# Masked attention over a sparse adjacency on one core: ScalarE's passes over three adj tiles, one search, one list of keys and one score put at other places in the order

## The chip, the cores and the metric

The kernel runs on one core of one Trainium2 chip. The metric is the device time in microseconds; lower is better. The kernel before took 669.54 us (median of three runs, 668.49 to 670.58). The program writes the order of work of ScalarE and VectorE by hand, and that of GpSimd in the first part; the order of the other queues (PE, the DMA queue of SyncE, GpSimd later) is made by a scheduler from the program's order and from what is ready.

## The reference

```python
h = relu(layernorm(x))                    # x: 2708 x 1024
q = h @ W_q.T + b_q;  k = h @ W_k.T + b_k;  v = h @ W_v.T + b_v
z = (q @ k.T) / 32
z = where(z * adj == 0, -10000, z * adj)  # adj: 2708 x 2708, 0 or 1, one in 677 set
out = x + relu(softmax(z) @ v)
```

A row of adj has four ones on average, so nearly all of the score matrix is masked.

## The kernel before

**Tiles and units.** The 2708 rows are 22 tiles of 128 (tile 21 has 20). The kernel first forms M, the product of the two score weights, on PE (lines 388 to 536). Then come 20 units, n = 0 to 19, of two tiles each: units 0 to 9 form score rows q = h M, units 10 to 19 the outputs from the summed rows u. One unit is a 2 x 2 block product with seven block multiplications of 8 matmuls each (`multiply`, `add_block` L909), and takes PE some 25.8 us. Within a unit, `after(i)` for i = 0 to 6 runs between the blocks: there the program places all other work. The results leave PSUM through ScalarE copies (L922, L925, L955, L987, L998) and VectorE sums (L990, L993 for q; L1020, L1024 for the outputs); the next unit's rows are transposed on PE (L359), copied by ScalarE (L649) and combined by VectorE (L653).

**The adj tiles.** Each is loaded by SyncE (L317, 1354 KB) into one of three buffers, tile t into buffer t mod 3. Three things are then done to it:

- `counted(t)` (L320, the pass): ScalarE adds up |adj| over each row (L324), the number of ones that the keys are held against at the end;
- `found(t)` (L326, the search): VectorE finds the places of the ones, four FIND_INDEX8 of 685 columns (L334);
- `listed(t)` (L336, the keys): for the last tile of a batch ((8..11), (16..19), (20), (21) are batches), VectorE turns the places of the batch into keys (L346 to L352).

The buffer is free for tile t + 3 when both the pass and the search have ended.

**The steps.** `steps_at[n, i]` (L700) is a string of steps that `follow` (L272) carries out in that order at `after(i)` of unit n. "p16" is the pass over tile 16, "i19" the search alone, "j19" the keys alone, "f16" search and keys (the keys only at a batch's end), "e9" pass, search and keys; the first step that names a tile asks for its load. "s", "r", "a", "h", "k" and "+" are steps of the layer norm of x: statistics on VectorE, root on GpSimd, application on ScalarE (L250), storing of h and the column sum on GpSimd. "c" is `counts(0, 11)`, "o" is `sort(0, 11)`, "w" writes the first table with GpSimd and ends GpSimd's order by hand (L297).

**Counts and sort.** `counts(11, 22)` runs at (3, 2): VectorE forms `hot` (L604) from the keys. `sort(11, 22)` at (3, 3) begins with two products of `hot` on PE (`ps_in` L615, `ps_all` L617), which stand in PE's queue ahead of a block of unit 3, and brings the rows in order of their number of ones, so that tile t needs only K[t] slots.

**Attention.** From unit 5 on, a generator, `attention` (L855), gives VectorE's steps for the sorted tiles in the order 8, 7, 6, 5, 4, 3, 2, 0, 1, 9, 15, 14, 13, 12, 16, 17, 20, 10, 18, 19, 11, and `advance` (L898) takes some 20 us of them per unit, by the costs that the steps yield. For a tile: `scores` (L784) is K[t] instructions L790, each on one gathered row of h (gathers by GpSimd, L545) and the tile's q rows; behind the last one, the q rows of the following tile are fetched. `weights` (L809) makes the softmax weights in a few small VectorE instructions (L832 to L834; L819 to L828 for tiles 10 and 20, which can hold rows without ones) and ends in one ScalarE instruction, the first term (L835; L829 for tiles 10 and 20). `sums` (L839) adds the other terms on VectorE (L843), and its first one waits for ScalarE. Where two neighbouring tiles have at most 12 slots together, two scores of the next tile go ahead of the weights and the rest between weights and sums. K is 2 for tiles 9, 10 and 20.

Of the kernel before, what the change touches and what calls it, by code (L numbers as in the profile page):

```python
# [39 lines left out]
def slot_counts(n, count):  # L40


    nodes = 2708
    pmf = [math.comb(nodes, k) * RATE**k * (1 - RATE) ** (nodes - k) for k in range(SLOTS + 1)]
    counts = []
    for t in range(count):
        k = 1
        while k < SLOTS:
            above = max(0.0, 1.0 - sum(pmf[: k + 1]))
            if n * above < 0.01 if t == 0 else n * above + 4 * math.sqrt(n * above * (1 - above)) <= t * P:  # L50
                break
            k += 1
        counts.append(k)
    return counts
# [3 lines left out]
def tile_preln_masked_attention(  # L58
# [24 lines left out]
    K = slot_counts(EARLY * P, EARLY) + slot_counts(N - EARLY * P, FULL - EARLY) + [0]  # L83
# [597 lines left out]
    def natural_rows(n):  # L681
# [15 lines left out]
    nc.vector.tensor_scalar(large[:, 0:1], large[:, 0:1], 10000.0, None, op0=ALU.is_gt)  # L697
    nc.vector.tensor_scalar(large[:, 1:2], large[:, 1:2], 250000.0 / D, None, op0=ALU.is_gt)

    steps_at = {(0, 0): "s4-5 e9", (0, 1): "r4 +0 +1 +2 f10", (0, 3): "p10 i11", (0, 4): "j11 a4 p11", (0, 5): "h4 +3 s6-7 e12",  # L700
                (0, 6): "r6 f13", (1, 1): "f14", (1, 2): "p13 a6", (1, 3): "h6 s8-9 p14", (1, 4): "r8 p15 i15", (1, 5): "j15",
                (1, 6): "f16 c", (2, 1): "f17", (2, 2): "p16 a8", (2, 3): "r10 f18 p17 w h8",
                (2, 4): "a10 p18", (2, 5): "f19 k10", (2, 6): "f20 f21 p19", (3, 2): "p20", (3, 3): "p21"}
    steps_ahead = {(2, 2): "o s10"}

    slots, free = [], []
# [44 lines left out]
    def ask(t):  # L751

        g_of[t] = []
        wanted.extend((t, s) for s in range(K[t]))

    def fetch(t):

        assert t in formed
        if t not in g_of:
            ask(t)  # L760
        tq[t] = work.tile([P, D], FT, tag="hT", name=f"pq_{t}", bufs=2)
        if t < EARLY:
            got = gather(tq[t], q_dram[:, :], t, SLOTS, P)
            if t == order[0]:
                first_q.append(got)
        else:
            nc.gpsimd.dma_start(tq[t], q_late[(t - EARLY) * P:(t - EARLY + 1) * P, :])

    def fill():
        while wanted and free:  # L770
            t, s = wanted.pop(0)
            g = free.pop(0)
            with tc.issue_after(first_q[0].ins) if first_q else nullcontext():
                gather(g, h_dram[:, :], t, s, P, skip=True)
            g_of[t].append(g)
# [8 lines left out]
    def scores(t, then):  # L784
        k = K[t]
        at[t] = list(range(k))
        for s in range(k):
            fill()
            junk = work.tile([P, D], mybir.dt.uint8, tag="junk", name="junk2", bufs=1)
            chained(lambda: nc.vector.scalar_tensor_tensor(  # L790
                junk, g_of[t][s], 1.0, tq[t], op0=ALU.mult, op1=ALU.mult, accum_out=zall[:, t, s:s + 1]))
            if s < k - WIDE:
                free.append(g_of[t][s])
            yield 1.3
        tq.pop(t)
        if k > WIDE:

            g_of[t] = g_of[t][k - WIDE:]
            wanted.extend((t, s) for s in range(k - WIDE))
            at[t] = list(range(k - WIDE, k)) + list(range(k - WIDE))  # L800
        if then is not None:
            fetch(then)
        fill()
        w = stat.tile([P, SLOTS + 1], FT, tag="w", name=f"w_{t}")
        if t not in EMPTY:
            nc.scalar.activation(w[:, :k], zall[:, t, 0:k], AF.Exp)
        ws[t] = w

    def weights(t):  # L809

        k = K[t]
        z, ok = zall[:, t, 0:k], valid[:, t, 0:k]
        w = ws.pop(t)
        m = stat.tile([P, 4], FT, tag="m", name=f"m_{t}")
        coef = stat.tile([P, SLOTS], FT, tag="coef", name="coef")
        u = row_tile(f"u_{t}")
        if t in EMPTY:
            assert summed
            nc.vector.memset(w[:, 0:1], MASKED)  # L819
            nc.vector.tensor_scalar(coef[:, :k], ok, -1.0, -MASKED, op0=ALU.add, op1=ALU.mult)  # L820
            nc.vector.tensor_mul(w[:, 1:1 + k], z, ok)
            nc.vector.tensor_add(w[:, 1:1 + k], w[:, 1:1 + k], coef[:, :k])
            nc.vector.tensor_reduce(m[:, 0:1], w[:, 0:1 + k], AX.X, ALU.max, negate=True)
            nc.scalar.activation(w[:, 0:1 + k], w[:, 0:1 + k], AF.Exp, bias=m[:, 0:1], accum_out=m[:, 1:2])
            nc.vector.scalar_tensor_tensor(m[:, 2:3], w[:, 0:1], float(N - 1 - k), m[:, 1:2], op0=ALU.mult, op1=ALU.add)
            nc.vector.reciprocal(m[:, 3:4], m[:, 2:3])
            nc.vector.tensor_scalar(coef[:, :k], w[:, 1:1 + k], w[:, 0:1], m[:, 3:4], op0=ALU.subtract, op1=ALU.mult)
            nc.vector.tensor_mul(m[:, 2:3], w[:, 0:1], m[:, 3:4])  # L828
            nc.scalar.activation(u, hsum, AF.Copy, scale=m[:, 2:3])  # L829
        else:  # L830
            with tc.issue_after(chain[-1].ins):
                nc.vector.scalar_tensor_tensor(w[:, :k], w[:, :k], 1.0, ok, op0=ALU.mult, op1=ALU.mult, accum_out=m[:, 1:2])  # L832
                nc.vector.reciprocal(m[:, 3:4], m[:, 1:2])
                chain.append(nc.vector.tensor_scalar(coef[:, :k], w[:, :k], m[:, 3:4], None, op0=ALU.mult))  # L834
            nc.scalar.activation(u, g_of[t][0], AF.Copy, scale=coef[:, at[t][0]:at[t][0] + 1])  # L835
            free.append(g_of[t][0])
        us[t] = u, coef

    def sums(t):  # L839
        u, coef = us.pop(t)  # L840
        for s in range(0 if t in EMPTY else 1, K[t]):
            fill()
            chained(lambda: nc.vector.scalar_tensor_tensor(  # L843
                u, g_of[t][s], coef[:, at[t][s]:at[t][s] + 1], u, op0=ALU.mult, op1=ALU.add))
            free.append(g_of[t][s])
            yield 1.3
        fill()
        g_of.pop(t)
        if near(t):
            held[t] = u  # L850
        else:
            nc.gpsimd.dma_start(u_dram[t * P:(t + 1) * P, :], u)
        done.add(t)

    def attention(order):  # L855
        for t in order[:2]:
            ask(t)

        fill()
        yield 0.0  # L860
        with tc.issue_after(chain[-1].ins):
            for lo, hi in parts:
                nc.vector.tensor_scalar(valid[:, lo:hi], ptab.bitcast(U32)[:, lo:hi, 0:SLOTS], float(N) - 0.5, NONE,
                                        op0=ALU.is_lt, op1=ALU.max)
        free.extend(slots[:8])
        fill()
        yield 0.0
        fetch(order[0])
        after = order[1:] + [None, None]
        yield from scores(order[0], after[0])  # L870
        for i, t in enumerate(order):
            nxt = after[i]
            ahead = nxt is not None and K[t] + K[nxt] <= HIGH + 1
            part = scores(nxt, after[i + 1]) if nxt is not None else iter(())
            if ahead:

                for _ in range(2):
                    yield next(part, 0.0)
            weights(t)
            yield 0.6  # L880
            if ahead:
                yield from part
            yield from sums(t)
            yield from part
# [4 lines left out]
    assert sorted(order) == list(range(FULL))  # L889
    chain = placed  # L890
    stream = attention(order)
    spent, now = [0.0], [0]

# [253 lines left out]
    for n, unit in enumerate(units):  # L1147
# [7 lines left out]
        nxt = units[n + 1] if n + 1 < len(units) else None  # L1155
# [123 lines left out]
    with tc.If(some > 0):  # L1279
# [19 lines left out]
        with tc.tile_pool(name="big", bufs=1, side="right") as big, tc.tile_pool(  # L1299
# [34 lines left out]
            with tc.For_i(0, NT) as i:  # L1334
# [35 lines left out]
                for b0 in range(0, N, NB):  # L1370
                    w = min(NB, N - b0)
# [84 lines left out]
```

## Time and profile before

| | |
|---|---|
| median of three runs | 669.54 us (668.49 to 670.58) |
| profiled execution | 670.24 us; span from first to last instruction 668.4 us |
| granted PE clock, mean | 0.993 |
| busy, us | PE 653.6, VectorE (DVE) 526.0, GpSimd (POOL) 401.4, ScalarE (ACT) 264.3 |
| moved | 193.24 MB, mean 289 GB/s |

How to read it: times are microseconds from the start of the span. L with a number is the line of the kernel that issued an instruction. `out<-in` names the tile written and those read: `adj` is an adj tile, `at` the places found in it, `sized` what the pass writes, `hot` the input of the sort, `junk` that of a score, `u` a sum of weighted rows. What stands behind "<-" in brackets is what ended an engine's idle time. A view of waits gives the total in us, the number and the longest. PEld is PE's weight load, and a name with q (SPq, POOLq) is an engine's DMA queue or sequencer.

### The profile page before, as it was taken

Reading aid. Unit: us, or ns where it says so; the run is one execution under the profiler, and the core shown is the slowest. Engines: PE = TensorE matmul, PEld = TensorE weight load, DVE = VectorE, ACT = ScalarE, POOL = GpSimd, SP = SyncE. Lnnn points to the kernel's source line nnn. Section 1 sums busy time; section 2 is a strip of 40 time slices with the busy share of each in tenths; the row PEclk is TensorE's granted clock in tenths of the full one; section 3 lists DMA queues with packets and bytes.
Section 4 is the critical chain, followed back from the end, with each engine's and each line's share of the span. In section 5 each row is a group of like instructions: output and inputs, shape, how many; then the busy total and the mean of one; then the engine's idle time right before and its main releaser. Section 6 shows DMA issues by size and latency. Waiting matters only on the chain.

```text
span 668.4 us, 6383 instructions
## 1 busy us (share of the span) xinstructions
PE 653.6 (98%) x1768; PEld 334.0 (50%) x1768; DVE 526.0 (79%) x1014; ACT 264.3 (40%) x395; POOL 401.4 (60%) x396
## 2 busy tenths in 40 slices
PE   7999999999998999999999999999999999999994
PEld 4777766444543444444444444444444444444441
DVE  5999879999887403988887999798798989989221
ACT  3467985765654212332241232432332433322200
POOL 2559991666476763775656365574674877873331
PEclk9999999999998999999999999999999999999998
DMA  8997989599575996897899999998997799895631
GB/s 345 408 360 259 371 302 377 220 400 340 207 222 171 343 374 219 276 393 240 312 312 351 382 417 390 305 302 252 325 299 193 235 296 364 220 278 170 147 121 66
DMA packets 62164, 193.24 MB, mean 289 GB/s; under 512 B 9689, under 2 KB 10041, under 8 KB 61226
## 3 DMA queue, kind: packets, MB, share of 16 engines
q0 software_dynamic: 34464, 109.25, 49.8%
q1 hardware_dynamic: 26650, 80.37, 32.5%
q10 hardware_dynamic: 1008, 3.15, 1.2%
q8 instruction: 16, 0.26, 0.2%
q14 instruction: 26, 0.21, 0.1%
HBM read 160.85 MB, written 44.93 MB: 308 GB/s over the span
## 4 chain that ended last, share of the span: by engine, by line
PE 79%; issue 5%; DMA 5%; DVE 5%; POOL 4%; ACT 2%; POOLq 0%; SPq 0%; DVEq 0%; ACTq 0%
PE ps L909 35%; PE psy L909 24%; PE ps_y L418 6%; PE ps_x L418 4%; PE ps_z L418 4%; PE pt L359 4%; POOL g L545 2%; DMA out_dram<-y,tab 2%; DMA adj<-in_adj_dram 2%; DVE junk L790 1%; DVE at L334 1%; POOL y L1008 1%; ACT sized L324 1%; DVE u L843 1%; DMA wlow<-in_wq_dram 1%
## 5 line engine op out<-in xcount | busy, mean ns | idle before, releaser
L545 POOL DMA_INDIRECT g<-h_dram,tab x104 | 125.1, 1203 | 54.5 <-issue 22.5
L909 PE MATMUL ps<-M,a 128*128 128x512 f32 x320 | 144.1, 593 | 0.1
L909 PE MATMUL psy<-wlow,s 128*128 128x512 f32 x320 | 144.1, 592 | 0.0
L790 DVE SCALAR_TENSOR_TENSOR junk<-g,pq 128x1024 uint8<-128x1024 f32 x92 | 112.6, 1224 | 2.3 <-DMA g<-h_dram,tab 0.4
L843 DVE SCALAR_TENSOR_TENSOR u<-g,coef,u 128x1024 f32<-128x1024 f32 x77 | 98.8, 1283 | 8.9 <-ACT u L835 7.3
L909 PEld LDWEIGHTS ps<-M,a 128*128 128x128 f32 x320 | 59.3, 190 | 68.0 <-issue 67.2
L909 PEld LDWEIGHTS psy<-wlow,s 128*128 128x128 f32 x320 | 59.2, 190 | 67.2 <-issue 67.2
L334 DVE FIND_INDEX8 at<-ones,adj 128x8 uint32<-128x685 f32 (+1 forms) x88 | 74.4, 866 | 0.0
L909 PE MATMUL ps<-M,s 128*128 128x512 f32 x160 | 73.6, 603 | 0.0
L909 PE MATMUL psy<-wlow,a 128*128 128x512 f32 x160 | 72.1, 593 | 0.4 <-DVE p L1020 0.4
L909 PE MATMUL ps<-wlow,s 128*128 128x512 f32 x160 | 71.9, 592 | 0.0
L324 ACT ACTIVATE sized<-adj 128x2708 uint8<-128x2708 f32 (+1 forms) x22 | 54.2, 2463 | 5.1 <-DMA adj<-in_adj_dram 5.0
L909 PEld LDWEIGHTS ps<-M,s 128*128 128x128 f32 x160 | 30.9, 194 | 38.4 <-issue 38.4
L1008 POOL DMA_INDIRECT y<-in_x_dram,tab x19 | 34.0, 1788 | 26.7 <-ACT y L1025 14.9
L909 PEld LDWEIGHTS psy<-wlow,a 128*128 128x128 f32 x160 | 30.2, 190 | 39.2 <-issue 34.6
L909 PEld LDWEIGHTS ps<-wlow,s 128*128 128x128 f32 x160 | 30.4, 190 | 38.3 <-issue 38.3
L259 POOL TENSOR_TENSOR hsum<-hsum,x 128x1024 f32<-128x1024 f32 (+1 forms) x17 | 40.3, 2370 | 0.3
L653 DVE TENSOR_TENSOR s<-a,pt 128x512 f32<-128x512 f32 x40 | 25.6, 681 | 15.5 <-ACT a L649 6.9
L649 ACT COPY a<-pt 128x512 f32<-128x512 f32 x60 | 33.2, 593 | 9.5 <-remote 3.7
L547 POOL DMA_INDIRECT pq<-q_dram,tab x11 | 14.6, 1329 | 33.5 <-DVE junk L790 16.3
L744 POOL DMA_INDIRECT out_dram<-y,tab x21 | 24.9, 1186 | 15.4 <-DMA y<-in_x_dram,tab 7.7
L545 POOL DMA_INDIRECT M<-h_dram,tab x20 | 27.0, 1350 | 10.1 <-issue 4.9
(236 smaller groups left out, 887.1 us busy)
## 6 DMA issues: line engine op xcount, KB each, us to landing
adj<-in_adj_dram SPq DMA_DIRECT2D x21, 1354.0 KB
x<-in_x_dram SPq DMA_DIRECT2D x21, 512.0 KB
h_dram<-x POOLq DMA_DIRECT2D x21, 512.0 KB
u_dram<-u POOLq DMA_DIRECT2D x14, 512.0 KB
or<-u_dram SPq DMA_DIRECT2D x14, 512.0 KB
q_late<-q SPq DMA_DIRECT2D x10, 512.0 KB
pq<-q_late POOLq DMA_DIRECT2D x10, 512.0 KB
g<-in_wv_dram SPq DMA_DIRECT2D x16, 256.0 KB
```

The costliest lines, as they stand in the source:

```text
L259: nc.gpsimd.tensor_add(hsum[:n], hsum[:n], xt[:n])
L324: nc.scalar.activation(sized[:n], a[:n, :, :PW], AF.Abs, accum_out=total[:n, t:t + 1])
L334: nc.vector.max_index(at[:n, t - first_t, g, :], ones[:n, 0:8], a[:n, g, :])
L359: nc.tensor.transpose(pt[:, c, :], xt[:, k * P:(k + 1) * P], ident)
L418: mm = nc.tensor.matmul(bank, a_tile(o + H * a[0], a[1], i), b(o), start=first and o == 0, stop=(o == H - 1), skip_group_check=True)
L545: return nc.gpsimd.indirect_dma_start(out=dst, out_offset=None, in_=src, in_offset=off, bounds_check=N - 1, oob_is_err=False)
L649: nc.scalar.copy(ops[name], bank)
L653: step = (eng or nc.vector).tensor_tensor(ops[name], a, b, op=op)
L790: chained(lambda: nc.vector.scalar_tensor_tensor(junk, g_of[t][s], 1.0, tq[t], op0=ALU.mult, op1=ALU.mult, accum_out=zall[:, t, s:s + 1]))
L843: chained(lambda: nc.vector.scalar_tensor_tensor(u, g_of[t][s], coef[:, at[t][s]:at[t][s] + 1], u, op0=ALU.mult, op1=ALU.add))
L909: mm = nc.tensor.matmul(bank, a[:, c, :], b[:, c, :], start=False, stop=(c == 3), skip_group_check=True)
L1008: return nc.gpsimd.indirect_dma_start(out=y[:n], out_offset=None, in_=x, in_offset=off, compute_op=ALU.add)
```

## The change

Three kinds of edit, in the table of steps and in `attention`:

- The passes over tiles 16, 17 and 18 go from (2, 2), (2, 3) and (2, 4) to (1, 6), (2, 2) and (2, 3).
- The search of tile 19 goes from (2, 5) to (2, 4), ahead of the sum L990 of unit 2; its batch's keys stay at (2, 5), behind that sum. The keys of tiles 8 to 11 go from (0, 4) to (0, 5), behind the sum L990 of unit 0.
- Where two scores of the next tile went ahead of the weights, it is now at most one fewer than its slots. With K = 2 one score is left for behind the weights; other tiles have three or more, and nothing changes for them.

```diff
-    steps_at = {(0, 0): "s4-5 e9", (0, 1): "r4 +0 +1 +2 f10", (0, 3): "p10 i11", (0, 4): "j11 a4 p11", (0, 5): "h4 +3 s6-7 e12",
+    steps_at = {(0, 0): "s4-5 e9", (0, 1): "r4 +0 +1 +2 f10", (0, 3): "p10 i11", (0, 4): "a4 p11", (0, 5): "j11 h4 +3 s6-7 e12",
                 (0, 6): "r6 f13", (1, 1): "f14", (1, 2): "p13 a6", (1, 3): "h6 s8-9 p14", (1, 4): "r8 p15 i15", (1, 5): "j15",
-                (1, 6): "f16 c", (2, 1): "f17", (2, 2): "p16 a8", (2, 3): "r10 f18 p17 w h8",
-                (2, 4): "a10 p18", (2, 5): "f19 k10", (2, 6): "f20 f21 p19", (3, 2): "p20", (3, 3): "p21"}
+                (1, 6): "f16 c p16", (2, 1): "f17", (2, 2): "p17 a8", (2, 3): "r10 f18 p18 w h8",
+                (2, 4): "i19 a10", (2, 5): "j19 k10", (2, 6): "f20 f21 p19", (3, 2): "p20", (3, 3): "p21"}
...
             if ahead:
 
-                for _ in range(2):
+                for _ in range(min(2, K[nxt] - 1)):
                     yield next(part, 0.0)
             weights(t)
```

## The prediction

> **What bounds the kernel.** I read the page first: TensorE (PE) is busy 653.6 of 668.4 us, so the kernel is PE plus its holes. The waits of PE alone name every hole; columns: us in total, times, longest.
>
> ```profile
> PE ps_y L453 <- POOL hsum L119: 2.8, 1, 2.8
> PE ps_in L615 <- DVE hot L604: 2.2, 1, 2.2
> PE ps_x L418 <- DMA wlow<-in_wq_dram: 0.8, 1, 0.8
> PE psy L909 <- DVE p L1020: 0.4, 1, 0.4
> ```
>
> The first and third lie in the first 6 us, which the change does not touch. Left are 2.2 us ahead of the sort of tiles 11 to 21 (`ps_in`) and 0.4 us late in the kernel. Next I cut the time around the 2.2 us into stretches (busy us of PE, PEld, DVE, ACT, POOL; then granted clock, DMA share, GB/s).
>
> ```profile
> 171.00:175.00 4.00, 4.00 (x19) 2.55 (x18) 3.79 (x11) 3.39 (x3) 0.00 (x0) 1.00 0.00 0
> ...
> 201.90:204.00 2.10, 0.00 (x0) 0.00 (x0) 1.67 (x8) 0.46 (x1) 0.99 (x2) 1.00 0.65 252
> 204.90:208.20 3.30, 3.30 (x6) 1.27 (x5) 3.16 (x7) 3.30 (x6) 0.43 (x1) 0.51 0.20 31
> ```
>
> PE is empty from 201.9 to 204.0, and then runs at half the granted clock for 3.3 us: the hole is paid twice. The reader should keep the first row in mind too: from 171 to 175 no DMA moves anything. The chain of work that ended last says why `hot` came late (start us, us, what).
>
> ```profile
> 181.83 10.94 DMA adj<-in_adj_dram
> 192.77 0.19 issue
> 192.95 3.48 DVE at L334 x5
> ...
> 197.60 3.37 DVE at L334 x4
> ...
> 203.52 0.38 DVE hot L604
> 203.90 0.14 issue
> 204.03 0.57 PE ps_in L615 x2
> ```
>
> So: load of adj tile 20, its search, keys, search and keys of tile 21, the counts, `hot`, PE. The load of 20 was issued at 181.83, because it goes into the buffer of tile 17 and ScalarE's pass over 17 (L324) had to end first. ScalarE's timeline:
>
> ```profile
> 172.68 2.47 ACT L324 ACTIVATE sized<-adj 128x2708 uint8<-128x2708 f32 x1
> ...
> 178.90 2.47 ACT L324 ACTIVATE sized<-adj 128x2708 uint8<-128x2708 f32 x1
> ...
> 187.70 1.24 ACT L250 ACTIVATE x<-x,r 128x1024 f32<-128x1024 f32 x1 [6.24 <-POOL r L241]
> 188.84 2.45 ACT L324 ACTIVATE sized<-adj 128x2708 uint8<-128x2708 f32 x1
> ```
>
> These are the passes over 16, 17 and 18, the last behind a 6.24 us wait. Tile 19 (buffer of 16) was issued at 175.26 and 21 (buffer of 18) at 191.41.
>
> **The passes a step up (p16, p17, p18).** Nothing is added; a pass is one ACTIVATE and the read of its accumulator, 2.56 us to the next start, and it issues no DMA, as f16 to f18 ask for those loads before it. p16 goes behind the copy L998 of unit 1 and its two stores, where ScalarE was free for the next copy at 167.88: it ends at 170.44. p17 takes p16's old place (172.68 to 175.2), p18 that of p17 (178.90 to 181.4), ahead of the 6.24 us wait. What p16 pushes on ScalarE: two copies L649, from 167.88 to 170.44, ending at 171.5, and with them their PSUM banks, which PE wants for the transposes at 171.56 and 172.0 (0.4 to 0.5 us to spare); L955 moves from 171.09 to about 171.5, and PE writes its bank next at 179.30. I cost both at nothing; without that cover PE would lose at most the 0.1 to 0.3 us of a semaphore.
>
> Loads: tile 19 can be issued at 170.5 instead of 175.26, into the empty DMA stretch above. It took 9.1 us before (175.26 until DVE started on it at 184.37): 179.6 at the latest. Tile 20 follows p17, 175.3 instead of 181.83; with the 11.1 us it took before, 186.4. Tile 21 follows p18, about 181.8 instead of 191.41. On SP the load of 20 passes the store of a q tile (issued 181.39), which waits for DVE's L993.
>
> **Search of 19 ahead of the sum L990, keys behind.** VectorE's order becomes: L993 until 181.25; search of 19, 3.37 us (as 18's, 177.28 to 180.65), 184.62; L990, 0.61, 185.23; keys of 16 to 19, 3.2 (187.87 to 191.07), 188.43; then search and keys of 20 and 21 and the counts, which ran from 192.95 to 203.89 without a gap worth naming, 10.94: **`hot` ends at 199.4 instead of 203.9.** The sum L990 ends 1.6 us later than before (183.6), but PE reads its bank at 189.60 only. PE comes to `ps_in` at 201.65 (block start 198.22 + 3.43), so 2.3 us are spare. Late next, then, is nothing but PE.
>
> Worth: before, the block behind the sort's two products starts at 204.82 and the one after it at 209.91. After, with the 0.67 us that the first sort's products took at 170.89, they start at 202.32 and 205.75. The gain is 4.16 us: 2.50 of hole and slow products, 1.66 of half clock.
>
> I book the 1.66 us because the trace has no other half-clock stretch between two busy ones. A rule that speaks against it: by the Trainium skill, "TensorE: Matmul & The Clock Gate", Part 1 (The HAM clock gate), the clock falls after an idle window of about 3.4 us, and this hole is shorter. By that rule the half clock need not go with the hole and the sum below would be 3.06 us, by the rows it is 4.72.
>
> **Keys of 8 to 11 behind a sum (j11).** In unit 0 the sum L990 ended at 137.20, behind 4.8 us of keys, and PE's next block took 3.58 us instead of 3.43 for it. With the sum first, at 131.7, PE gets **0.15 us**. The keys then push bn_stats and searches by 0.6 us; 1.13 us of waiting for an adj load at 147.86 take that up.
>
> **A score kept for behind the weights.** It differs where the next tile has two slots: 9 behind 1, 20 behind 17, 10 behind 20. No instruction is added; one score (L790, 1.22 us) moves into the time in which VectorE waits for ScalarE's first term. With it the fetch of the following tile's q rows, which POOL issues behind the last score, comes 0.7 us later (what the weights' small steps take); at 534.83 it was 7.7 us ahead of the first score that reads it (542.55), so I cost that at nothing. The waits:
>
> ```profile
> 535.69 1.30 DVE L843 SCALAR_TENSOR_TENSOR u<-g,coef,u 128x1024 f32<-128x1024 f32 x1 [1.22 <-ACT u L835]
> ...
> 548.61 1.28 DVE L843 SCALAR_TENSOR_TENSOR u<-M,coef,u 128x1024 f32<-128x1024 f32 x1 [1.22 <-ACT u L829]
> ...
> 571.81 0.69 DVE L1020 TENSOR_TENSOR p<-psy,p 128x512 f32<-128x512 f32 x1
> ```
>
> The third place (424.46, 1.28 us) is worth nothing: VectorE waits for PE soon after (1.51 us at 433.00). In these two, VectorE has no wait for PE between 510.36 and 571.81, so 2.44 us come out of the run that ends in L1020, the 0.4 us hole of PE. **0.41 us**; the other 2 us find PE busy.
>
> **Does the front gain reach the end?** PE has no hole from 205 to 572, so a lead of 4.3 us lasts as long as the others follow. VectorE waited for PE in every unit up to 510 (1.51 us at 484.57, 1.28 at 510.36), so it comes along; its waits for gathers come to some 0.4 us over 92 scores. DMA was at 0.92 of its time from 300 to 400 and 0.94 from 400 to 476: not full.
>
> **Sum:** 4.16 + 0.15 + 0.41 = 4.72 us. The profiled execution took 670.24 (span 668.4), 0.7 above the median of 669.54 and inside 668.49 to 670.58. So 665.5 for such an execution, and 669.54 - 4.72 = **664.8 us** for the median.
>
> **Rivals.** A measurement of this kernel can tell about 0.3%, 2.0 us, from no change.
>
> A. The forecast, 664.8: **0.64**.
>
> B. The load of 20 stays behind the q store, so that the change does not do what it says. SP's order is not written by hand, and before it was store, then load. Landing at 192.9 again, `hot` is at 203.9 again: 669.54 - 0.56 = 669.0. Against it: then both became free within 0.2 us of each other; now the load is free 6 us earlier. It decides from a landing of 190.7 on, microsecond for microsecond. **0.08**.
>
> C. The half clock stays though the hole goes: 669.54 - (2.50 + 0.15 + 0.41) = 666.5. For it: the 2.8 us hole at the start (first fence) shows no half clock in the records, so a hole of this length need not bring it. Against: it stands right behind the 2.2 us hole and nowhere else. **0.08**. The skill's rule above is on this side.
>
> D. The lead is lost at L1020, because VectorE from 510 on is held by POOL's gathers and not by PE. The chain there does run through POOL's queue. PE would wait 0.41 + 4.31 - 2.44 = 2.28 us, perhaps with 1.66 of half clock: a gain of 2.4 or 0.8, 667.1 to 668.8. **0.08**.
>
> E. Slower. POOL's queue behind the first table's write (step w) is ordered by a scheduler, not by hand, and changed readiness may reorder it. At 504.31 to 511.99 it stood 7.68 us before a gather-add that waited for ScalarE's y. Gathers for the scores from 521 on put behind such a wait would make VectorE 7.68 later: PE waits 0.41 + 7.68 - 2.44 = 5.65, with half clock 7.31, in place of 0.41, against the lead of 4.31: +2.6, 672.1. It decides (slower by 2.0) from a delay of 7.1 us. Against it: the edits change no transfer's size, and POOL's order is written by hand up to w. **0.12**.
>
> Range: the runs before spread by about 1 us either side, and gains larger than the sum have no source, so 663.4 below; above it takes in C and D, 668.8. Outside lie B and E, 0.20. Faster by over 0.3% (below 667.5): A, C and a quarter of D, 0.74; within: B and the rest of D, 0.14; slower 0.12.
>
> **What would show it.** Right: the pass over 16 between 167.9 and 170.5; adj loads issued near 170.5, 175.3 and 181.8; search of 19 ahead of L990 and no DVE wait on adj after 181; no PE wait on `hot`; no half clock before the end; no PE wait on L1020; waits on L829 and L835 near 548 and 536 (less the lead) gone. Wrong: a load of 20 still near 181.8, a half clock near 203, or a PE hole near 568 longer than 0.4 us.

## The result, and the profile after

The changed kernel took **666.67 us** (median of 22 runs, 665.12 to 673.73), the kernel before beside it 670.24 us (22 runs, 667.94 to 671.68). The ratio is 0.9956, with a 95% interval of 0.994 to 0.9971: faster by 0.44%, or 2.9 us (1.9 to 4.0). The forecast was 664.8 us, a gain of 4.72. On the forecast's base of 669.54 us the ratio makes 666.6 us: inside its range, with 0.6 of the gain. The profiled execution took 666.55 us with a span of 664.8, where 665.5 was forecast for it.

The waits of PE in the changed kernel; columns: us in total, times, longest.

```profile
PE ps_y L453 <- POOL hsum L119: 2.8, 1, 2.8
PE ps_x L418 <- DMA wlow<-in_wq_dram: 0.8, 1, 0.8
PE pt L359 <- DVE sort L619: 0.2, 1, 0.2
```

By this list both holes that the change was priced on are gone, `hot` and L1020 (0.2 us of the first are left, as shown below). A small new one has come: transposes (L359) that wait for VectorE's copy out of the first sort (L619). The stretches that the prediction showed, in the same columns (busy us of PE, PEld, DVE, ACT, POOL; then clock, DMA share, GB/s):

```profile
171.00:175.00 4.00, 3.81 (x19) 2.22 (x18) 3.83 (x11) 2.43 (x5) 0.00 (x0) 1.00 0.68 216
201.90:204.00 2.10, 2.06 (x8) 1.12 (x7) 2.03 (x7) 1.33 (x3) 1.56 (x2) 1.00 0.50 199
204.90:208.20 3.30, 3.30 (x9) 1.39 (x8) 3.23 (x4) 1.84 (x2) 2.16 (x2) 1.00 0.63 214
```

The DMA engines, empty in the first stretch before, now move 216 GB/s there: tile 19 is loaded early. PE is busy through the other two, at full clock. ScalarE's three passes stand where the diff puts them:

```profile
168.29 2.46 ACT L324 ACTIVATE sized<-adj 128x2708 uint8<-128x2708 f32 x1 [0.52 <-DVE sort L599]
...
174.35 2.47 ACT L324 ACTIVATE sized<-adj 128x2708 uint8<-128x2708 f32 x1
...
180.57 2.47 ACT L324 ACTIVATE sized<-adj 128x2708 uint8<-128x2708 f32 x1
```

The loads of 19, 20 and 21 were issued at 170.88, 176.93 and 183.16, and VectorE waited for none of them. But `hot` came later than the forecast of 199.4. VectorE's instructions, and then GpSimd's add, beside one of them:

```profile
192.67 0.19 DVE L346 TENSOR_TENSOR cand<-first,at 128x32 f32<-128x32 f32 x1
...
197.22 2.83 DVE L346 TENSOR_TENSOR cand<-first,at 20x32 f32<-20x32 f32 x1
...
202.16 0.37 DVE L604 TENSOR_TENSOR hot<-deg,down 128x198 f32<-128x198 f32 x1
```

```profile
197.62 2.38 POOL L259 TENSOR_TENSOR hsum<-hsum,x 128x1024 f32<-128x1024 f32 x1
```

The same instruction L346 took 0.19 us at 192.67 and 2.83 at 197.22, on a smaller tile; it ended at 200.05, with GpSimd's add (200.00). `hot` ended at 202.53, and `ps_in` started 0.14 us behind it, at 202.67, as far behind as in the kernel before. The block in front of it had started at 199.03. Where nothing holds PE, the next instruction starts 3.44 us after such a start (198.08 and 201.52 in e7_both below); here that would be 202.47. So of the forecast 2.3 us to spare nothing was left, and PE lost 0.2 us. The list of waits doesn't show them, because the profile counts the block as busy until 202.63.

### The profile page after: what moved, and what is told of

Same layout as the page of the kernel before. It is cut to its first block, busy times and chain, and to the rows that moved or that the text cites. A ratio compares the mean times of both kernels' runs of the same rounds, so it can differ in the third digit from the quotient of the medians.

```text
span 664.8 us, 6378 instructions
## 1 busy us (share of the span) xinstructions
PE 652.3 (98%) x1768; PEld 333.4 (50%) x1768; DVE 529.5 (80%) x1014; ACT 263.6 (40%) x395; POOL 403.4 (61%) x396
## 4 chain that ended last, share of the span: by engine, by line
PE 90%; DVE 4%; DMA 3%; ACT 2%; issue 0%; POOL 0%; POOLq 0%; ACTq 0%
PE ps L909 42%; PE psy L909 28%; PE ps_y L418 6%; PE pt L359 5%; PE ps_x L418 5%; PE ps_z L418 4%; DMA adj<-in_adj_dram 2%; DVE at L334 2%; DMA wlow<-in_wq_dram 1%; ACT sized L324 1%; ACT a L649 0%; DVE st L212 0%; ACT x L250 0%; PE ps_h L1114 0%; PE ps_v L530 0%
## 5 line engine op out<-in xcount | busy, mean ns | idle before, releaser
L909 PE MATMUL ps<-M,s 128*128 128x512 f32 x160 | 71.9, 592 | 0.0
L259 POOL TENSOR_TENSOR hsum<-hsum,x 128x1024 f32<-128x1024 f32 (+1 forms) x17 | 40.3, 2371 | 0.4
L653 DVE TENSOR_TENSOR s<-a,pt 128x512 f32<-128x512 f32 x40 | 25.6, 680 | 14.6 <-ACT a L649 14.6
L744 POOL DMA_INDIRECT out_dram<-y,tab x21 | 27.2, 1294 | 15.4 <-DMA y<-in_x_dram,tab 7.5
L649 ACT COPY a<-pt 128x512 f32<-128x512 f32 x60 | 33.2, 592 | 5.3 <-PE pt L359 5.3
L545 POOL DMA_INDIRECT M<-h_dram,tab x20 | 24.9, 1245 | 12.0 <-DMA h_dram<-x 5.2
```

Source lines behind the costliest of these rows:

```text
L259: nc.gpsimd.tensor_add(hsum[:n], hsum[:n], xt[:n])
L545: return nc.gpsimd.indirect_dma_start(out=dst, out_offset=None, in_=src, in_offset=off, bounds_check=N - 1, oob_is_err=False)
L649: nc.scalar.copy(ops[name], bank)
L744: to = nc.gpsimd.indirect_dma_start(out=out, out_offset=bass.IndirectOffsetOnAxis(ap=ptab.bitcast(U32)[:n, t, SLOTS:SLOTS + 1], axis=0), i ...
L909: mm = nc.tensor.matmul(bank, a[:, c, :], b[:, c, :], start=False, stop=(c == 3), skip_group_check=True)
```

## The experiments

Times are medians, with the lowest and highest and the number of runs. Ratios are to the kernel before, run beside them on the same chip; it took 669.31 us (32 runs) beside e1 to e4, 669.59 (18 runs) beside a_after to e7, and 670.74 (18 runs) beside the last four.

| | us | ratio, 95% interval | profiled span |
|---|---|---|---|
| e1_front | 668.04 (666.03 to 672.12, 11) | 0.9972 (0.9951 to 0.9992) | 666.8 |
| e2_score | 668.56 (666.98 to 670.24, 12) | 0.9989 (0.9975 to 1.0002) | 666.0 |
| e3_passes | 666.50 (666.11 to 668.13, 10) | 0.9959 (0.9945 to 0.9973) | 664.5 |
| e4_search | 668.55 (667.77 to 671.19, 12) | 0.9998 (0.9982 to 1.0015) | 666.4 |
| a_after | 667.36 (665.41 to 668.04, 7) | 0.9959 (0.9938 to 0.998) | 666.3 |
| e5_p16_behind | 666.48 (665.69 to 673.14, 12) | 0.9987 (0.9957 to 1.0016) | 664.2 |
| e6_adds_later | 666.03 (664.82 to 667.58, 6) | 0.9942 (0.9923 to 0.9961) | 664.2 |
| e7_both | 665.24 (664.74 to 666.03, 6) | 0.993 (0.9914 to 0.9947) | 663.5 |
| c_p16 (e5 again) | 672.57 (666.54 to 674.21, 12) | 1.0016 (0.9988 to 1.0043) | 671.3 |
| c_both (e7 again) | 667.02 (665.18 to 669.93, 7) | 0.9939 (0.9917 to 0.9961) | 668.2 |
| b_before, b_before2 | 669.0 and 670.39 (one run each) | | 667.2, 668.7 |

**e1_front**: passes and search of 19 alone; the keys of 8 to 11 and the score stay where they were.

```diff
-                (1, 6): "f16 c", (2, 1): "f17", (2, 2): "p16 a8", (2, 3): "r10 f18 p17 w h8",
-                (2, 4): "a10 p18", (2, 5): "f19 k10", (2, 6): "f20 f21 p19", (3, 2): "p20", (3, 3): "p21"}
+                (1, 6): "f16 c p16", (2, 1): "f17", (2, 2): "p17 a8", (2, 3): "r10 f18 p18 w h8",
+                (2, 4): "i19 a10", (2, 5): "j19 k10", (2, 6): "f20 f21 p19", (3, 2): "p20", (3, 3): "p21"}
```

> The passes over 16 to 18 and the search of 19 alone; keys of 8 to 11 and the scores as before. Theory: the gain is the hole ahead of the sort. PE then has no wait on hot and no half clock, its blocks behind ps_in come 3.9 us earlier against those ahead of it (as in the kernel after), 0.4 us are lost at 171 to 174 where PE's transposes wait for the sort, and the 0.4 us wait of PE on L1020 is there again: time 2.7 to 3.6 us below before. Rival (the score is what pays): under 1.5 us below before.

Most of the gain is here, and the wait for `hot` is gone from the list. But PE waited 2.0 us for L619, ten times as long as in the changed kernel's profile, and gave a part of the gain back. The two edits left out need not be the reason: a_after below has all edits and the same wait.

**e2_score**: the third edit alone.

```diff
-                for _ in range(2):
+                for _ in range(min(2, K[nxt] - 1)):
```

> The score kept for behind the weights alone. Theory: PE's hole of 2.2 us and the half clock stay; the only change on PE is that the 0.4 us wait on L1020 goes, so 0.4 us below before, which the times can't tell from none. Rival (VectorE held the kernel from 510 on): two ScalarE waits of 1.2 us leave VectorE and the end comes 2.4 us earlier.

PE's wait on L1020 is gone. With the block behind it, which was slower before, PE gained 0.6 us there in this profile; the rival's 2.4 us did not come, and the interval of the ratio reaches to no change. VectorE's three waits for ScalarE's terms between 505 and 575 (3.6 us) became one (1.2). The front is that of before, with a wait of 2.0 us for `hot`, but at 204.70 to 208.00 the clock is 1.00 and not 0.51:

```profile
201.80:203.80 2.00, 0.15 (x1) 0.00 (x0) 1.79 (x10) 1.81 (x4) 0.87 (x2) 1.00 0.48 183
204.70:208.00 3.30, 3.30 (x9) 1.48 (x8) 3.16 (x7) 1.36 (x2) 0.09 (x1) 1.00 0.41 87
```

This is the first sign against the forecast's 1.66 us of half clock.

**e3_passes**: the passes alone, with search and keys of 19 together at (2, 5).

```diff
-                (1, 6): "f16 c", (2, 1): "f17", (2, 2): "p16 a8", (2, 3): "r10 f18 p17 w h8",
-                (2, 4): "a10 p18", (2, 5): "f19 k10", ...
+                (1, 6): "f16 c p16", (2, 1): "f17", (2, 2): "p17 a8", (2, 3): "r10 f18 p18 w h8",
+                (2, 4): "a10", (2, 5): "f19 k10", ...
```

> The passes alone; the search of 19 stays behind L990. L990 waits for PE until 183 and the search begins at 183.6 instead of 182.2, so hot comes about 1.4 us later than in the kernel after, where it had 0.04 us to spare: a PE hole of 1.4 us. If a hole of that length brings the half clock too (the gap makes it), the blocks behind ps_in gain 0.8 us against before; if it does not, 2.5 us. The times then lie 0.4 or 2 us below before.

As fast as the whole change, with no wait for `hot` (it ended at 201.61) or L619. The expected hole of 1.4 us did not come: VectorE came to L346 of tile 21 at 198.24, 1.0 us later than in the changed kernel, but by then GpSimd's add had run since 196.71, and L346 took 0.90 us and not 2.83. The passes bring the gain.

**e4_search**: the search of 19 alone, the passes as before.

```diff
-                (2, 4): "a10 p18", (2, 5): "f19 k10", (2, 6): "f20 f21 p19", (3, 2): "p20", (3, 3): "p21"}
+                (2, 4): "i19 a10 p18", (2, 5): "j19 k10", (2, 6): "f20 f21 p19", (3, 2): "p20", (3, 3): "p21"}
```

> The search of 19 ahead of L990 alone; the passes as before. The loads of 19 and 20 stay at 175.3 and 181.8, so the search of 20 begins near 192.9 and hot ends near 203.9 as before: no gain, within 0.5 us of before, half clock there. L990 ends near 188.4, still ahead of PE's block at 189.6. Rival (the order on VectorE is the lever, the loads are not): hot 3 us earlier.

No gain. The load of 20 was issued at 181.87 as before, VectorE waited 2.75 us for it, and PE's hole stayed:

```profile
192.85 0.09 DVE L334 MATCH_VALUE_LOAD at<-ones,adj 128x8 f32 x1 [2.75 <-DMA adj<-in_adj_dram]
```

```profile
PE ps_in L615 <- ACT ps L678: 1.8, 1, 1.8
```

The profile names ScalarE's L678, which came at the same time; `hot` ended at 203.57, and `ps_in` started 0.14 us behind it, as before.

**a_after**: the changed kernel again, beside the next three.

> The kernel after once more, beside the three that follow: 2.5 to 4 us below before; PE waits for hot 0.0 to 0.1 us; L346 of tile 21 and one L653 stretched to about 3 us beside a GpSimd add.

The ratio repeats. The new hole does not: 1.9 us in place of 0.2. PE's wait, and the start of VectorE's search of tile 14 (f14 at (1, 1)):

```profile
PE pt L359 <- DVE sort L619: 1.9, 1, 1.9
```

```profile
150.35 0.09 DVE L334 MATCH_VALUE_LOAD at<-ones,adj 128x8 f32 x1 [2.84 <-DMA adj<-in_adj_dram]
```

In the changed kernel's other profile that search began at 148.78. VectorE does not make up for the 1.57 us before L619, and PE waits 1.7 us longer there. In e1 the search began at 150.26. The load of 14 itself was issued at 132.4 to 133.6 in every profile; its landing varies.

**e5_p16_behind**: the changed kernel, with the pass over 16 behind ScalarE's two copies L649.

```diff
-                (1, 6): "f16 c p16", (2, 1): "f17", ...
+                (1, 6): "f16 c", (2, 0): "p16", (2, 1): "f17", ...
```

> The kernel after with the pass over 16 put behind the two copies L649 of unit 2 instead of ahead of them. Theory: the pass ahead of the copies is why PE's order changed at 171 (transposes between halves of a block, the first waiting for the sort's L619); with it behind, PE's order there is that of before, the 0.4 us come back, and the load of 19 is issued some 1.1 us later, which its search does not notice. 0.4 us below the kernel after on PE. Rival (the earlier loads change that order): PE's order stays as in the kernel after.

PE's order at 172 is that of before again, no L619 wait is left, and 8 of 12 runs took 665.69 to 666.77. The other four took 671.95 to 673.14, with a mean clock of 0.990 to 0.993: a stall that this profile does not hold. It was caught later (c_p16).

**e6_adds_later**: the changed kernel, with GpSimd's adds (L259) of the h tiles of the last groups put off ("k" keeps an h tile and leaves its add for later).

```diff
-  (2, 3): "r10 f18 p18 w h8",
+  (2, 3): "r10 f18 p18 w k8",
```

> The kernel after with the column sums of h tiles 8 and 9 put off on GpSimd until behind the row gathers. Theory: the 2.83 us L346 and the 3.23 us L653 come from GpSimd's adds L259 running beside them; without the adds both take their usual 0.2 and 0.7 us, hot ends near 200 and PE gets to ps_in 2 us behind it: 0.2 to 0.3 us below the kernel after on PE. Rival (DMA traffic or the small tile slows them): the two stay long.

With no add on GpSimd between 170 and 205, L346 has its usual length and `hot` ends at 199.46, where the prediction had 199.4:

```profile
196.81 0.18 DVE L346 TENSOR_TENSOR cand<-first,at 20x32 f32<-20x32 f32 x1
...
199.09 0.37 DVE L604 TENSOR_TENSOR hot<-deg,down 128x198 f32<-128x198 f32 x1
```

**e7_both**: e5 and e6 together.

```diff
-                (1, 6): "f16 c p16", (2, 1): "f17", (2, 2): "p17 a8", (2, 3): "r10 f18 p18 w h8",
+                (1, 6): "f16 c", (2, 0): "p16", (2, 1): "f17", (2, 2): "p17 a8", (2, 3): "r10 f18 p18 w k8",
```

> Both of these in the kernel after: 0.6 to 0.7 us below the kernel after on PE, the sum of the two; 4.5 us below before plus or minus the start. Rival (their gains overlap, or GpSimd's later adds hold the gathers of the first scores): no better than the better one of the two.

The lowest time of all, 665.24, with no wait of PE but the two at the start. Its ratio's interval (up to 0.9947) still touches that of the changed kernel beside it (from 0.9938).

**b_before, b_before2**: the kernel before, unchanged, for two more profiles.

> The kernel before, unchanged, for a second profile of it. Theory: the hole ahead of the sort (PE waiting for hot) is in every execution, 1.8 to 2.3 us, but the half-clock stretch behind it is not: of 50 runs of the kernel before beside the other experiments 10 had a mean granted clock of 0.993 and took 1.1 to 1.5 us more than the other 40. So most likely (4 in 5) this profile shows the hole, no half clock near 205, a mean clock of 0.996 and about 669 us. Rival: every hole of 2.2 us brings half clock: a stretch of 3.4 us near 205, clock 0.993, 670.2 us.

> A third profile of the kernel before, with the same expectation as the second: a hole of 1.8 to 2.3 us for hot, and a half-clock stretch behind it only if the mean clock is 0.993. A hole whose length differs by over 0.5 us between the profiles would say that the landing of tile 20 varies, and that the 2.50 us of the prediction is no fixed number either.

Both show a wait of 2.3 us for `hot`. Behind it, first b_before, then b_before2:

```profile
205.00:208.40 3.40, 3.40 (x11) 1.73 (x10) 2.55 (x5) 3.40 (x6) 1.16 (x1) 1.00 0.49 156
```

```profile
204.90:208.40 3.50, 3.50 (x7) 1.61 (x6) 2.74 (x5) 3.50 (x5) 1.16 (x1) 0.57 0.47 148
```

The same hole of the same kernel brought the half clock in one execution (mean clock 0.993) and not in the other (0.997).

**c_p16**: e5 again.

> The kernel with the pass over 16 behind the copies, a second time. Before, 4 of its 12 runs took 672 to 673 us with a mean clock of 0.990 to 0.993, the other 8 about 666.2. Theory 1: the stall belongs to where the pass stands: again some 3 in 10 of the runs above 671. Theory 2: it is a rare event of any of these kernels (of the changed kernel 2 of 22 runs, of the kernel with both edits none of 6): at most 1 in 10 here, median 666.0 to 666.6, ratio to the kernel before 0.994 to 0.996.

Nine of 12 runs were above 672, and the profile holds the stall. PE's wait; then VectorE, GpSimd, and the clock behind:

```profile
PE ps_in L615 <- DVE hot L604: 5.1, 1, 5.1
```

```profile
198.16 2.37 DVE L346 TENSOR_TENSOR cand<-first,at 20x32 f32<-20x32 f32 x1 [0.46 <-issue]
...
202.42 3.80 DVE L603 TENSOR_SCALAR deg<-deg 128x11 f32<-128x11 f32 x1
206.25 0.36 DVE L604 TENSOR_TENSOR hot<-deg,down 128x198 f32<-128x198 f32 x1
```

```profile
198.11 2.36 POOL L259 TENSOR_TENSOR hsum<-hsum,x 128x1024 f32<-128x1024 f32 x1
202.08 1.16 POOL L580 DMA_DIRECT2D tab<-tab_dram  x1 [1.61 <-DMA tab_dram<-tab,pos_i]
...
203.84 2.35 POOL L259 TENSOR_TENSOR hsum<-hsum,x 128x1024 f32<-128x1024 f32 x1
```

```profile
206.90:210.00 3.10, 3.10 (x7) 2.07 (x8) 3.03 (x6) 0.65 (x2) 0.00 (x0) 0.50 0.81 264
```

Two instructions on the way to `hot` were held until an add of GpSimd ended: L346 to 200.53 (add 200.47), and L603, 0.17 or 0.18 us in every other profile but c_both, to 206.22 (add 206.19). Tile 14's search had also begun late, at 149.29. PE was there at 206.76 - 5.1 = 201.66, where the prediction had it (201.65). The clock was halved from 204.9 to 211.7.

L603 is what sets this execution apart, and a race decides on it. In all six profiles with the passes moved and the adds in place, L603 begins 1.95 us behind the end of the first add. GpSimd's next instruction, L580, which reads the table back, waits until the table's writes have landed. It began 1.96 to 2.44 us behind that end in five of them, and 1.61 here, so L580, a store's issue and the second add were ahead of L603. In the changed kernel's first profile L603 was through before:

```profile
201.95 0.17 DVE L603 TENSOR_SCALAR deg<-deg 128x11 f32<-128x11 f32 x1
```

```profile
202.44 1.16 POOL L580 DMA_DIRECT2D tab<-tab_dram  x1 [2.44 <-DMA tab_dram<-tab,pos_i]
```

Of the executions above 671 us only this one has a profile. Neither theory forecast so many: 13 of 24 runs with the pass behind the copies, and 2 of 29 of the changed kernel. Why this kernel loses the race so often is open.

**c_both**: e7 again.

> The kernel with both later edits (pass over 16 behind the copies, GpSimd's adds later), a second time. Theory: 665.2 again (664.7 to 666.0), ratio 0.992 to 0.995, no PE wait but those of the start, hot near 199.9. Rival: it shares the stall of the kernel with the pass over 16 behind the copies, and some of its runs take 671 to 673.

The ratio is as expected, the median (667.02) above the expected 664.7 to 666.0, as was the kernel before beside it (670.74). Six of the seven runs took 665.18 to 667.72, and the profile is of the seventh (669.93, clock 0.993). Tile 14's search began at 150.73, and L346 began 1.98 us late for a cause that the profile does not name:

```profile
201.13 0.18 DVE L346 TENSOR_TENSOR cand<-first,at 20x32 f32<-20x32 f32 x1 [1.98 <-remote]
```

L603 took 0.71 us here: L580 had begun 0.38 us ahead of it, and no add stood behind. PE waited 2.1 us, and the half clock followed. In the 19 runs without the adds (e6, e7 and here) the stall of 672 to 674 us did not come, but a late tile 14 still costs. What held L346 stays open; ScalarE's L955 also had an idle time until 201.26 that the profile puts down to no engine.

## Why the prediction was right, and where it was not

**The passes bind, and moving them removes the hole: right.** e3 has the gain without the other edits, e4 has none with the load of 20 where it was. All three loads went out 0.4 to 1.6 us behind the forecast times, and the q store went behind the load of 20 (B did not happen). The load of 20, taken as 11.1 us, was no limit: VectorE did not wait for it.

**1.66 us of half clock: the step that was mis-sized.** The prediction booked it in full because the one profile had it. Of the 68 runs of the kernel before beside the experiments, 20 had a mean clock of 0.993 or less, the mark of that stretch in the three profiles of it. So it is worth about 1.66 x 20/68 = 0.5 us on average (0.3 to 0.9 us by the three groups of runs), and rival C's reason ("a hole of this length need not bring it") was right for most executions. The forecast took a single execution for the median. What C says did not happen, though: in the seven profiles in which the hole went, the clock is 1.00 behind `ps_in`, and only 2 of the 22 runs of the changed kernel had so low a mean clock. That its price, 666.5 us, lies next to the measured 666.67 is luck, and so is the nearness of the 3.06 us by the skill's rule to the measured 2.9. By that rule a hole this short leaves the clock alone; two profiles of the kernel before show the half clock behind 2.2 and 2.3 us, and they decide. The Trainium skill, "TensorE: Matmul & The Clock Gate", Part 1, also says that the activity window runs freely, so that the number of slow matmuls at a kernel's start differs from run to run; here a slow stretch in mid-kernel differs in this way, in the two profiles of before above.

**2.3 us to spare for `hot`: wrong.** The forecast `hot` (199.4) assumed every VectorE instruction at the length that it had before. Before, GpSimd's two adds stood at 180.33 and 184.00; with the passes moved the scheduler put them at 197.62 and 204.19, behind the 11 writes of the table. e6, which takes them out, ends `hot` at 199.46. The profile that the prediction read shows such a hold: the same L346, on tiles of the same size, takes 0.29 us alone and 0.89 beside an add of GpSimd that ends at 160.50.

```profile
159.77 0.89 DVE L346 TENSOR_TENSOR cand<-first,at 128x128 f32<-128x128 f32 x1
...
187.87 0.29 DVE L346 TENSOR_TENSOR cand<-first,at 128x128 f32<-128x128 f32 x1
```

```profile
158.14 2.36 POOL L259 TENSOR_TENSOR hsum<-hsum,x 128x1024 f32<-128x1024 f32 x1
```

A second part is tile 14's landing: the search began between 147.0 (or earlier, without a wait) and 150.73 in these profiles, and VectorE is late by as much. For c_p16 the parts make 199.4 + 1.43 (tile 14) + 0.46 + 2.19 (L346) + 3.63 (L603) = 207.1, 0.5 us more than the measured 206.61. The prediction used one landing, 147.86, as if it were fixed.

**The pass over 16 at no cost: wrong.** The prediction bounded it at 0.1 to 0.3 us of a semaphore, for copies that end before PE needs the bank. It did not see that the scheduler would split PE's transposes and set them behind VectorE's L619. PE lost 0.41 us there in the profile of the changed kernel, and 2.1 us in a_after. In e3 and e6 the same order cost nothing, because L619 came in time; e5 and e7 restore the old order and have no such wait. (A pass also takes 2.45 us to the next start in the rows, not 2.56, which changes nothing.)

**The two small terms: right, the second a little low.** PE gained 0.15 us at 137 (keys of 8 to 11), and L1020's hole of 0.4 us went, in the changed kernel and in e2; with the slower block behind it PE gained 0.63 us. Rival D did not happen: the lead reached L1020.

**E, slower through GpSimd's queue: not so in the changed kernel, but near.** A reordering did come, not among the gathers but of two adds, and it acts through VectorE. In c_p16 the median rose to 672.57, 1.8 us above the kernel before beside it, but the ratio's interval takes in no change, and by another mechanism than E's: that E said 672.1 is luck. One of the changed kernel's 22 runs took 673.73 with a clock of 0.991, as c_p16's do; what happened in it was not seen.

**The sum.** The profiled pair differs by 670.24 - 666.55 = 3.69 us. Block by block, the changed kernel's PE starts 0.56 us later (a block at 109.10 instead of 108.54), gains 0.15 at 137, loses 0.41 at the split, gains 3.87 ahead of the block at 206.85 and 0.63 at L1020: 3.68 in all. The 3.87 stand for the forecast's 4.16: 1.65 of half clock, as booked, and 2.22 of hole and products instead of 2.50, because `hot` was late. In e6 and e7, without the adds, the front gains 4.15. For the median the terms are 2.22 to 2.50, 0.5, 0.15 and 0.41 to 0.63, less the 0.4 to 2.1 us that the two profiles of the changed kernel lose at L619: 1.2 to 3.4 us, and the ratio says 2.9 (1.9 to 4.0). How often each length of the L619 wait occurs is open.

## What to carry to other kernels

A price read from one profile is a sample: before a hole's side effect (a half clock, a landing) is booked, look at whether the mean clock and the times of the other runs show it in all of them. Slack on an engine is only slack if nothing on its path is stretched by what another engine does meanwhile; when a move lets a scheduler reorder GpSimd, look at what VectorE runs beside it. And where a cover of half a microsecond hides a moved instruction, ask for the order that the scheduler makes of the queue behind it, not only for the times.

## What the runs showed of the hardware

Some VectorE instructions that take 0.17 to 0.7 us elsewhere took up to 3.8 us beside an add of GpSimd, and ended with it: L346 (0.18 and 2.83) and L603 (0.17 and 3.80). L653 of `s` and `a` went from 0.68 to 3.23 in the changed kernel and ended 0.56 us behind the add at 204.19. The hold is no effect of the change: in b_before and b_before2 L346 of tiles 16 to 19 took 0.95 and 1.09 us beside an add, and 0.28 or 0.29 in the other profiles. The sums L993 and L990, which have one input in PSUM, kept 0.67 and 0.69 us beside the add from 182.24 to 184.58 in b_before.

The Trainium skill, "SBUF — State Buffer", section "Who interferes with whom", says that a VectorE instruction with two inputs in SBUF contends with a GpSimd instruction that reads SBUF, that whoever issues first keeps the shared ports for the whole instruction while the other is blocked, and that a VectorE instruction with a single SBUF input outside the two-port modes does not contend; L346, L653 of `s` and `a` and the two sums agree. Which of the two issued first can't be read from the records: the held L346 has the earlier start (197.22, the add 197.62). L603 has one SBUF input, and no run here shows in which mode it ran. It was held in the two profiles in which GpSimd's L580 had begun before it, in c_both with no add behind.

A hole of PE of 2.1 to 2.3 us was followed by half the clock in three profiles of four (two of the three of the kernel before), one of 1.8 to 2.0 us in none of four, and one of 5.1 us in the one profile that has it. The slow stretch lasted 3.4 us in the three, and 6.8 in the last, the first 1.9 us of them inside the hole.
